# Zero products also into banks that a step will start anew, and another table of due times

## The chip, the cores and the metric

The kernel runs on one core of one Trainium2 chip. The metric is the device time of one execution in microseconds. The kernel before took 186.7 us, the median of three runs (185.85, 186.70 and 187.02).

## The reference

Inputs are `x` (4096 x 64, f32), an adjacency matrix `adj` (4096 x 4096, f32, zeros and ones), a weight (64 x 64) and a bias (64). What is computed:

```python
h = jnp.maximum(_layernorm(x, axis=-1), 0.0)
support = h @ weight
mask = (adj != 0).astype(support.dtype)
rank = jnp.cumsum(mask, axis=1)
deg = rank[:, -1:]
k = jnp.minimum(deg, 100.0)
pos = rank - (deg - k)
w = mask * jnp.where(pos > 0, 0.5 ** (k - pos), 0.0)
return x + (w @ support + bias)
```

So the last neighbour of a row has weight 1, the one ahead of it 1/2, and so on, up to 100 neighbours. `adj` is 64 MiB of the 68.19 MB that the kernel reads, and each element of it has to be turned into a weight before the large product.

## The kernel before

The rows of `adj` are handled in 32 tiles of 128 rows and 4096 columns, 2 MB each. Tiles 0, 1 and 28 to 31 are loaded in two or three pieces (`CUTS`), the others in one. A tile passes through these steps, each a small function:

- `load` (SP's queue) brings it into one of four buffers `a_sb`. It has to wait until the convert of the tile four before has read that buffer.
- `convert` (DVE, L563) makes bytes of the 0/1 numbers, in two halves of 2048 columns; `flip` (DVE, L573) transposes them in blocks of 32.
- `totals` (PE, L581) counts neighbours in blocks, `split` (ACT, L589) copies the counts to `sums`, `suffix` (PE, L602) sums them over all later blocks, `clamp` (DVE, L608) limits the result, `place` (PE, L618 and L622) adds the ranks within a block. `place` fills four banks of PSUM with exponents.
- `weigh` (ACT, L636), four per tile, reads one such bank each and writes the weights `wk` by an exponential. For one quarter of tiles 30 and 31 DVE does this instead (`encode`, L643, and `take`, L647).
- `aggregate` (PE, L656) multiplies the weights of a pair of tiles with `hr`, the support in two parts, in eight steps of four matmuls, adding up in a bank. A bank takes two pairs, that is a group of four tiles (the last group uses two banks).
- `drain` (ACT L671 or DVE L673) takes a finished group out of its bank, `turn_back` (PE, L679) transposes it, `finish` (DVE, L685) adds `x`, `store` writes it out.

Ahead of this, in the first 50 us, a setup computes the layer norm and the support: `turn`, `center`, `spread`, `support` on PE, `turned`, `square`, `relu`, `first` on ACT, `root`, `power`, `scale` (L532), `second` (L542) on DVE.

**The order of the steps.** There is no loop over tiles in the emitted program. `tasks` lists 665 steps with engine, estimated hold and lag, and needs; `plan` puts them in order. At each turn it takes the first open step of every kind, finds when each could start, and among those of the engine with the earliest that can start within `WAIT` (250 ns on PE, 60 on DVE, 150 on ACT, 60 on POOL, 0 on SP) of it, takes the one with the smallest due time from `DUE`. Steps of one kind keep their order. Each engine then runs its steps strictly in the planned order. `plan` also picks the banks: a step that writes a fresh bank gets the one that is free the earliest, and the bank numbers go to it as `homes`.

**Zero products.** `plan` asks for a number of products of zeros ahead of a step on PE, from PE's gap before the step and from the rows it streamed in the last 3.4 us:

```python
idle = max(0, min(int((at - end) * 0.6) // 110, (4200 - recent) // 256))
```

`warm` (L482) issues them: 128 x 256 products of the zero tile `junk` (L484). They need a bank to write. `idle` names it: at first the last bank; after an aggregate the bank and columns of that aggregate, to which zeros are added. A `drain` of the bank that `idle` names empties `idle` (L668), and from then on to the next aggregate `warm` issues nothing.

## Time and profile before

| | |
|---|---|
| median of three runs | 186.7 us |
| the profiled execution, its own time | 187.01 us |
| its span, first to last instruction | 185.0 us |
| busy in the span: PE, DVE, ACT | 165.2, 153.9, 149.5 us |
| DMA, mean over the span | 376 GB/s |
| DMA, 10 to 160 us | some 425 GB/s |
| mean granted TensorE clock | 0.98 |

The span is cut in 40 slices, each a digit of busy tenths for each engine. Groups of instructions carry the line of the kernel, the engine, the output and input tile, the count, the mean time of one, and the idle time just before them with what ended it. A wait written as `[0.33 <-PE bank L581]` means that the engine was idle for 0.33 us and that a PE instruction of line 581 released it.

### The profile page before, as it was taken

The numbers are of one execution on the slowest core, as the hardware profiler recorded it, in microseconds if no ns is written. First come the engines' busy times: TensorE is split into PE (matmuls) and PEld (weight loads), VectorE is DVE, ScalarE is ACT, GpSimd is POOL, SyncE is SP. The second block draws the span as 40 slices with busy tenths as digits, with TensorE's granted clock in tenths as the row PEclk, the third lists the DMA queues.
The fourth block names the chain that finished last, engine by engine and source line by source line (L and its number), as shares of the span: only waits on it lengthen the run. The fifth ranks groups of instructions, "written<-read, shape, count | busy, mean of one in ns | idle before, by whom it ended". The sixth has DMA issues, their size and how long they took to land.

```text
span 185.0 us, 4842 instructions
## 1 busy us (share of the span) xinstructions
PE 165.2 (89%) x2087; PEld 128.4 (69%) x2087; DVE 153.9 (83%) x204; ACT 149.5 (81%) x196; POOL 7.7 (4%) x43
## 2 busy tenths in 40 slices
PE   7999987579799999899999899997499999989992
PEld 5857874267586776687868588776277678777891
DVE  6667299999999999898889698888984989998731
ACT  2476912839699999999999999994896999999931
POOL 7810000000000000000000000000000000000000
PEclk9999999999999999999999999999958999999999
DMA  6999999999999999999999999999999999960020
GB/s 225 420 415 436 429 425 418 441 407 446 414 436 418 427 425 418 436 429 425 425 422 432 418 429 432 418 432 425 429 422 420 413 416 416 414 267 0 4 87 28
DMA packets 6807, 69.55 MB, mean 376 GB/s; under 512 B 898, under 2 KB 1154, under 8 KB 2178
## 3 DMA queue, kind: packets, MB, share of 16 engines
q1 hardware_dynamic: 6786, 69.24, 89.1%
q8 instruction: 16, 0.26, 0.6%
q14 instruction: 5, 0.04, 0.1%
HBM read 68.19 MB, written 1.05 MB: 374 GB/s over the span
## 4 chain that ended last, share of the span: by engine, by line
ACT 29%; PE 26%; DMA 19%; DVE 16%; issue 8%; SPq 0%; ACTq 0%; DVEq 0%
ACT wk L636 23%; DMA a_sb<-in_adj_dram 19%; PE bank L656 15%; DVE m L563 8%; ACT sums L589 4%; PE bank L602 4%; DVE mt L573 3%; PE bank L679 3%; PE bank L622 2%; PE bank L581 2%; PE bank L618 2%; DVE behind L608 1%; DVE wk L532 1%; DVE hr L542 1%; ACT acc_sb L671 1%
## 5 line engine op out<-in xcount | busy, mean ns | idle before, releaser
L636 ACT ACTIVATE wk<-bank 128x1024 fp32r<-128x1024 uint8 (+2 forms) x136 | 122.7, 1067 | 7.9 <-PE bank L622 6.3
L563 DVE TENSOR_SCALAR m<-a_sb 128x2048 uint8<-128x2048 f32 (+1 forms) x66 | 85.7, 1345 | 14.5 <-DMA a_sb<-in_adj_dram 14.3
L656 PE MATMUL bank<-wk,hr 128*128 128x256 f32 x512 | 73.2, 292 | 3.5 <-DVE hr L542 2.5
L656 PEld LDWEIGHTS bank<-wk,hr 128*128 128x128 f32 x512 | 64.4, 192 | 10.3 <-issue 5.0
L573 DVE STREAM_TRANSPOSE mt<-m 128x1024 f32<-128x1024 f32 (+2 forms) x40 | 40.5, 1022 | 0.4
L589 ACT ACTIVATE sums<-bank 128x512 f16<-128x512 uint8 x32 | 21.6, 685 | 7.2 <-PE bank L581 7.2
L608 DVE TENSOR_SCALAR behind<-bank,excess 128x256 f16<-128x256 f32 x32 | 14.8, 466 | 4.4 <-PE bank L602 4.1
L602 PEld LDWEIGHTS <-far 128*128 128x128 f16 x224 | 17.7, 99 | 0.9
L602 PE MATMUL bank<-sums,far 128*128 128x224 f16 (+6 forms) x224 | 18.1, 222 | 0.0
L618 PE MATMUL bank<-behind,where 32*128 32x256 f16 x256 | 14.5, 277 | 3.9 <-DVE behind L608 1.9
L484 PE MATMUL bank<-junk 128*128 128x256 bf16 x93 | 14.7, 299 | 1.2 <-DVE junk L372 1.2
L581 PE MATMUL bank<-mt,band 128*32 128x256 f16 x256 | 13.3, 284 | 2.4 <-DVE mt L573 1.7
L622 PE MATMUL bank<-mt,tri 32*32 32x512 f16 x512 | 14.4, 403 | 0.0
L602 PE MATMUL bank<-sums,near 128*128 128x256 f16 x32 | 9.0, 280 | 4.4 <-ACT sums L589 3.8
L484 PEld LDWEIGHTS <-junk 128*128 128x128 bf16 x93 | 9.0, 106 | 4.8 <-issue 2.0
L618 PEld LDWEIGHTS <-where 32*128 32x128 f16 x256 | 4.7, 92 | 9.8 <-issue 7.4
L581 PEld LDWEIGHTS <-band 128*32 128x32 f16 x256 | 4.5, 95 | 7.9 <-issue 3.8
L622 PEld LDWEIGHTS <-tri 32*32 32x32 f16 x512 | 4.4, 88 | 6.9 <-issue 6.9
L602 PE MATMUL bank<-sums,rest 128*128 128x256 f16 x32 | 8.8, 276 | 0.0
L495 ACT ACTIVATE wk<-bank 64x512 f32<-64x512 f32 x8 | 4.3, 587 | 4.9 <-PE bank L491 4.9
L685 DVE TENSOR_TENSOR xr<-bank,xr 128x256 f32<-128x256 f32 (+1 forms) x9 | 3.5, 389 | 5.6 <-PE bank L679 5.6
L679 PE MATMUL bank<-both,acc_sb 128*128 128x64 f32 x56 | 7.5, 277 | 0.6 <-ACT acc_sb L671 0.6
(95 smaller groups left out, 86.2 us busy)
## 6 DMA issues: line engine op xcount, KB each, us to landing
a_sb<-in_adj_dram SPq DMA_DIRECT2D x26, 2048.0 KB, 16.8
a_sb<-in_adj_dram SPq DMA_DIRECT2D x10, 1024.0 KB, 12.7
a_sb<-in_adj_dram SPq DMA_DIRECT2D x4, 512.0 KB, 14.5
xr<-in_x_dram SPq DMA_DIRECT2D x2, 512.0 KB, 4.8
out_dram<-xr SPq DMA_DIRECT2D x1, 512.0 KB
out_dram<-xr SPq DMA_DIRECT2D x1, 384.0 KB, 2.7
out_dram<-xr SPq DMA_DIRECT2D x2, 64.0 KB, 1.6
w<-in_L_gnn_weight_dram SPq DMA_DIRECT2D x2, 16.0 KB, 9.4
```

The source lines that it names most:

```text
L484: nc.tensor.matmul(idle[0][:, idle[1]:idle[1] + 2 * P], junk[:, :P], junk, start=not accs, stop=not accs, skip_group_check=True)
L563: nc.vector.tensor_scalar(words[n][:, k0 * P:k1 * P, :].rearrange("p (h q) e -> p h e q", q=P), tiles[t][:, (h0 + k0) * W:(h0 + k1) * W].r ...
L573: nc.vector.transpose(to[:, h0:h1], m_v.rearrange("p (h c l) -> p h c l", c=4, l=SUB))
L581: nc.tensor.matmul(tot[SUB * c:SUB * (c + 1), r], band[:, SUB - 12 - 4 * a:2 * SUB - 12 - 4 * a], masks[t][:, c, r, a], start=(a == 0), st ...
L589: nc.scalar.activation(sums8[t][:, :, r], pts.pop((n, "n")).bitcast(U8).rearrange("p (i f) -> p f i", f=4)[:, :2, r], AF.Copy, bias=-136.0)
L602: nc.tensor.matmul(o, l, m, start=(k == 0), stop=(k == len(todo) - 1), skip_group_check=True)
L608: nc.vector.tensor_scalar(behind[n][:, r], pts.pop((n, "s"))[:, r], excess, float(MAX_NEIGH), op0=ALU.subtract, op1=ALU.min)
L618: nc.tensor.matmul(vs[n, j][:, h0:h1, a, :], where[q, a, :], behind[n][q, r], start=(a == 0), stop=False, skip_group_check=True)
L622: nc.tensor.matmul(vs[n, j][SUB * c:SUB * (c + 1), h0:h1], tri[q, q], masks[t][q, c, r, :].rearrange("p (h r) a -> p h a r", r=SUB), start ...
L636: nc.scalar.activation(to[:, :, :, j, :], v[:, :2, x], AF.Exp, scale=-LN2, bias=-38.0 * LN2)
L656: nc.tensor.matmul(accs[g][:, at:at + 2 * P], hr[:, h * 4 + e, :, :].rearrange("p s d -> p (s d)"), wts[u][:, s, 2 * h + a].rearrange("p i ...
L679: nc.tensor.matmul(pts["o", d][:, k, :], sums[d][:, k * P:(k + 1) * P], both, start=True, stop=True)
```

## The change

Two things. First, `warm` no longer stops when `idle` is empty: it then writes its zero products into the first bank of `homes`, the one that the step about to be issued will start anew. To make this possible `homes` is set before `warm` is called. Such products start and stop an accumulation of their own, as those ahead of the first aggregate do. A step without banks of its own still gets none. Second, nearly all due times in `DUE` are others; costs, needs, buffers and the rule of `plan` are as they were. The orders of loads against fetches and of the stores don't change. Of the table only the kinds spoken of below are shown; numbers stand in the order of tiles, for `weigh` four to a tile (more for tile 29, and three per part for tiles 30 and 31).

```diff
@@ DUE @@
...
-    "split": [468, 298, 398, 367, 301, 306, 338, 385, 365, 389, 267, 369, 215, 291, 184, 201, 206, 274, 271, 261, 263,
-    401, 335, 319, 295, 293, 322, 379, 381, 414, 356, 357],
+    "split": [484, 337, 322, 377, 314, 383, 333, 416, 320, 415, 267, 400, 233, 325, 240, 289, 304, 362, 366, 301, 356,
+    381, 251, 262, 264, 252, 265, 293, 360, 358, 359, 363],
-    "totals": [445, 418, 94, 112, 489, 84, 87, 138, 140, 144, 130, 118, 119, 208, 256, 229, 86, 221, 168, 228, 186, 165,
-    145, 164, 197, 179, 49, 45, 63, 71, 73, 479],
+    "totals": [451, 428, 127, 129, 477, 130, 122, 218, 195, 205, 153, 136, 111, 200, 229, 155, 154, 199, 159, 167, 160,
+    117, 175, 80, 62, 61, 75, 59, 68, 46, 112, 49],
-    "suffix": [467, 463, 120, 111, 487, 139, 106, 141, 98, 126, 128, 107, 193, 207, 200, 157, 161, 174, 247, 250, 163,
-    212, 205, 198, 177, 236, 55, 66, 69, 76, 51, 650],
+    "suffix": [464, 458, 219, 173, 491, 208, 152, 183, 124, 179, 158, 143, 228, 238, 214, 191, 184, 215, 168, 178, 115,
+    87, 84, 81, 55, 106, 101, 78, 64, 99, 102, 121],
-    "weigh": [505, 216, 243, 342, 321, 325, 328, 361, 312, 307, 302, 355, 366, 387, 373, 374, 386, 364, 354, 399, 396,
-    394, 362, 345, 392, 340, 384, 280, 390, 391, 284, 276, 242, 189, 265, 289, 375, 219, 241, 257, 292, 204, 255, 187,
-    283, 297, 290, 190, 203, 211, 282, 270, 252, 259, 264, 268, 275, 244, 262, 269, 281, 287, 273, 285, 266, 246, 346,
-    334, 279, 288, 327, 278, 332, 260, 402, 339, 337, 348, 314, 331, 341, 299, 351, 336, 311, 320, 310, 376, 308, 318,
-    323, 315, 294, 316, 329, 317, 304, 248, 305, 330, 382, 417, 286, 296, 370, 406, 383, 388, 371, 393, 377, 416, 359,
-    368, 350, 358, 378, 395, 352, 372, 405, 412, 397, 347, 353, 333, 349, 403, 413, 343, 415, 407, 410, 344, 411, 409],
+    "weigh": [577, 298, 174, 340, 417, 344, 405, 336, 423, 329, 222, 406, 422, 413, 379, 328, 424, 394, 235, 378, 420,
+    425, 371, 312, 427, 334, 242, 271, 419, 414, 278, 309, 389, 280, 206, 319, 426, 286, 316, 305, 421, 318, 225, 310,
+    373, 375, 317, 221, 330, 313, 243, 321, 307, 306, 376, 323, 295, 367, 353, 303, 352, 396, 324, 351, 302, 392, 402,
+    365, 395, 409, 407, 374, 245, 382, 390, 404, 380, 279, 254, 263, 244, 297, 261, 290, 283, 284, 288, 268, 250, 269,
+    259, 277, 258, 253, 270, 266, 247, 273, 274, 294, 276, 272, 296, 275, 339, 255, 327, 368, 361, 364, 372, 369, 335,
+    341, 357, 393, 355, 370, 349, 391, 397, 398, 347, 403, 331, 332, 388, 401, 399, 346, 350, 385, 345, 342, 387, 348],
...
@@ -480,8 +480,11 @@
     idle = [banks[BANKS - 1], 2 * P]
 
     def warm(n):
-        for i in range(n if idle else 0):
-            nc.tensor.matmul(idle[0][:, idle[1]:idle[1] + 2 * P], junk[:, :P], junk, start=not accs, stop=not accs, skip_group_check=True)
+
+        to = idle or [banks[i] for i in homes[:1]] + [0]
+        for i in range(n if len(to) > 1 else 0):
+            keep = bool(idle and accs)
+            nc.tensor.matmul(to[0][:, to[1]:to[1] + 2 * P], junk[:, :P], junk, start=not keep, stop=not keep, skip_group_check=True)
 
     pxs, ns = {}, {}
 
@@ -693,8 +696,8 @@
         support, scale, first, second, convert, flip, totals, split, suffix, clamp, place, weigh, encode, take, aggregate,
         drain, turn_back, finish, store)}
     for at, spare, f, args, given in plan():
+        homes[:] = given
         warm(spare)
-        homes[:] = given
         does[f](*args)
 
     last = {}
```

Of the other kinds, `power` goes from 495 to 507, `scale` from 500, 454, 449, 507 to 504, 476, 472, 509.

## Prediction

> **What bounds the kernel now.** I read the slices of the page first, for the engine that is full in each stage and for the clock.

> ```profile
> PE   7999987579799999899999899997499999989992
> ...
> ACT  2476912839699999999999999994896999999931
> ...
> PEclk9999999999999999999999999999958999999999
> DMA  6999999999999999999999999999999999960020
> ```

> One digit is 4.6 us. Loads fill the DMA engines up to slice 35 and end in the 36th. ACT is full from about 50 us on, but for slices 28 to 31. PE has a dip in slices 28 and 29 (124.9 to 134.1 us), and right after it the only dip of its clock. So I cut that stretch into steps of 3.4 us; columns are length, then busy time (count) of PE, weight loads, DVE, ACT and POOL, then clock, DMA share and GB/s.

> ```profile
> 124.90:128.30 3.40, 3.40 (x41) 2.96 (x41) 2.48 (x3) 2.01 (x4) 0.00 (x0) 1.00 1.01 424
> 128.30:131.70 3.40, 1.85 (x56) 0.75 (x57) 3.40 (x6) 1.43 (x2) 0.00 (x0) 1.00 1.01 429
> 131.70:135.10 3.40, 1.49 (x14) 1.33 (x11) 3.37 (x3) 3.40 (x5) 0.00 (x0) 0.74 1.00 424
> 135.10:138.50 3.40, 3.40 (x20) 2.56 (x20) 2.86 (x4) 3.07 (x5) 0.00 (x0) 0.50 1.00 424
> 138.50:141.90 3.40, 3.40 (x45) 2.47 (x45) 0.81 (x3) 2.72 (x4) 0.00 (x0) 0.75 1.00 424
> ```

> PE is half idle from 128.3 to 133.7; then it is fully busy at half clock until about 140. Finer steps put the half clock from 133.7 to 140.1, 6.4 us, so 3.2 us of PE's work are lost. In it ACT and DVE starve. From the timeline of ACT, three waits on PE, and of DVE one:

> ```profile
> 136.70 0.60 ACT L589 ACTIVATE sums<-bank 128x512 f16<-128x512 uint8 x1 [0.33 <-PE bank L581]
> 139.81 2.86 ACT L636 ACTIVATE wk<-bank 128x1024 fp32r<-128x1024 uint8 x3 [0.68 <-PE bank L622]
> 143.68 0.60 ACT L589 ACTIVATE sums<-bank 128x512 f16<-128x512 uint8 x1 [1.01 <-PE bank L581]
> ...
> 141.36 0.48 DVE L608 TENSOR_SCALAR behind<-bank,excess 128x256 f16<-128x256 f32 x1 [2.59 <-PE bank L602]
> ```

> ACT loses 0.33 + 0.68 + 1.01 = 2.02 us. After 144.3 it has no hole above 0.2 us until its last weigh ends at 177.58, though the last load lands at about 166.4 (the DMA share falls to zero there). So ACT, with PE some microseconds behind it, sets the end, not the loads; 2 us lost at 140 are 2 us at 185.

> Ahead of the dip ACT has a larger hole of another origin:

> ```profile
> 130.27 2.85 ACT L636 ACTIVATE wk<-bank 128x1024 fp32r<-128x1024 uint8 x3 [3.36 <-PE bank L622]
> ```

> split(21) stands on ACT behind all four weighs of tile 20. Only then can suffix, clamp and place of tile 21 run, one after another on PE, DVE and PE, before ACT has a weigh again. PE idles in the same hole, and that costs the clock.

> **Why PE had no filler there.** The planner's rule, followed through for the kernel before, asks for 108 zero products; the page has 93:

> ```profile
> L484 PE MATMUL bank<-junk 128*128 128x256 bf16 x93 | 14.7, 299 | 1.2 <-DVE junk L372 1.2
> ```

> The missing 15 are 2 ahead of place(21), 3 ahead of totals(23) and 10 ahead of suffix(23). drain(4), at 125.74 on ACT, clears `idle`, and it stays empty until aggregate(10, 0), at 134.84 in the trace. They fall just into the stretch that loses its clock.

> [...] here the starts of `near` and `rest` (256 columns) at 127.53 and 127.64 are 110 ns apart. [...]

> **The change, part by part.**

> Filler allowed after a drain: were the order as before, 15 products more. At 110 ns they are 1.65 us of PE. Ten lie ahead of suffix(23), 1.1 us, inside PE's wait of 1.91 us for `sums`; the others lie in PE's waits of 1.11 and 0.44 us. Cost: nothing while those waits and a free bank cover it; if the bank is read late, up to 1.1 us for the ten. They raise PE's work in 131.7 to 135.1 from 1.49 to about 2.6 us, and some earlier. That it suffices is my choice: from 30 to 40 us PE is busy 6.67 of 10 us, 2.3 in 3.4, at clock 1.00. Gain: the 2.02 us of ACT, bounded by 0 (it doesn't suffice) and by PE's 3.2 us. The 3.36 us hole stays: the new table still gives split(21) 381 against 244 to 297 for the weighs of tile 20.

> What is late next: the landing. The last convert (0.73 us) could start at 166.4 instead of 167.81, so flips end 1.4 us sooner than 169.2, at 167.8. clamp(30), behind them, takes 0.48, place(30) 0.7, then ACT needs 3 x 1.03 us for weigh(30) before tile 31: 167.8 + 0.5 + 0.7 + 3.1 + 0.2 of gaps is 172.3, against 174.34 now. So the tail can follow by 2.0 us and hardly more, which is also what ACT gives.

> Order: the diff changes nearly every due time, no duration, and the fetches, loads and stores keep their order on SP. A due time decides only between steps that can start within 250, 60, 150 or 60 ns (PE, DVE, ACT, POOL) of the earliest, so most of the order follows the data. Counting from the tables where split(n) is due after every weigh of tile n-1: tiles 2, 3, 9, 11, 13, 21, 29, 31 before; 9 and 21 after. That is fewer chances for a hole. In the tail totals(31) goes from due 479 to 49 and suffix(31) from 650 to 121, ahead of most aggregates; in the trace they stood 1.1 us (168.99 to 170.11, eight matmuls of L656) and 0.5 us behind such. Together 1.6 us at most, but weigh(30) on ACT covers it except for the gaps of 0.16 and 0.17 us before the last split and weigh. I count 0.2 us. A loss is open too: the trace of before can't bound how the new order fills 20 to 50 us, where ACT is busy only 16.55 of 30 us. I bound it by one tile of ACT work either way: 4 x 1.067 + 0.685 = 4.95 us.

> Sum: 2.0 + 0.2 = 2.2 us off a span of 185.0, so 182.8. Around the span lie 2.0 us (187.0 - 185.0). That execution is 0.3 us above the median of the three, so against 186.7 the forecast is 184.5 us.

> **The rivals.**

> One: the clock is repaired and the tail closes up (45%): 184.5, its own range 183.6 to 185.6; 185.6 is half the gain.

> Two, slower: a later ramp of ACT (27%). Place: 20 to 50 us, where DVE is full (27.68 of 30 us) and ACT waits for DVE's scale (3.58 and 2.64 us) and for hr (1.39 us). If setup steps there are ordered so that one tile's ACT work slips past 50 us, 4.95 us come on top of a stage in which ACT is full; 186.7 - 2.2 + 4.95 = 189.5. It decides against the change as soon as ACT's busy time in 20 to 50 falls by more than 2.2 us. For it: DVE is saturated there, and new due times for every tile's convert against scale and second. Against: these steps keep similar ranks (power 495 to 507, scale 449-507 to 472-509).

> Three: no effect (16%): the half clock comes all the same, in this hole or another, with the waits unchanged: 186.7, give or take 1. [...]

> Four: the order also closes the 3.36 us hole, and clamp(30) gets ahead of the last flips (12%). Then place(31) limits: flips at 167.8 plus totals 0.4, split 0.6, suffix 0.75, clamp 0.5, place 0.75 and 0.5 of gaps is 171.3, instead of 174.25: 3.0 off, 183.7; if ACT also ramps earlier no more, as the landing holds. Order of DVE in the last 5 us could give another 0.7: 183.

> **How the numbers follow.** 1% is 1.9 us, about what a measurement of this kernel can tell from no change: faster is below 184.8, slower above 188.6. Case one puts 60% below 184.8 (27) and the rest within (18); case four is all faster (12); case two is 24 slower and 3 within; case three is 14 within and 1 each side. Faster 40%, same 35%, slower 25%. The range from 183.2 to 189.5 leaves out the upper half of case two and a little of case four.

> **What would show it.** Right: PEclk without a dip; L484 above 93, some of them writing banks between a drain and the next aggregate; ACT's waits on PE in 130 to 145 gone; the last weigh ends near 175.5. Wrong: ACT's busy time in 20 to 50 below 14.4 us; a dip in another slice; zero products directly ahead of a step with a wait on a bank's reader; L563 waiting for a buffer rather than for DMA, or a DMA slice below 400 GB/s before 160 us, which would mean that loads waited for DVE.

## The result and the profile after

The changed kernel takes 184.76 us (median of four runs, 184.69 to 184.88) against 186.86 us for the kernel before (185.85 to 187.05); the ratio is 0.990, 95% interval 0.986 to 0.994. The span of the profiled execution is 182.8 us, 2.2 less than before. The kernel before spreads more than the changed one: in the later rounds below its median lay between 185.94 and 186.49 us, so 1.5 us is as fair a size of the gain as 2.1.

The slices of the page of the changed kernel, 4.57 us each:

```profile
PE   7999999598899899989999898997999989999992
...
ACT  2576801928999999999999999649999999999931
PEclk9999699969999999999999999999999999999999
DMA  6999999999999999999999999999999999992020
```

The dip of the clock behind 130 us is gone. There is one in slice 5 and another in slice 9, in the setup, where the kernel before had none in its profiled execution. ACT still has a hole, now in slices 26 and 27, some 9 us earlier than before.

The same steps of 3.4 us as in the prediction, for the changed kernel, with the same columns:

```profile
124.90:128.30 3.40, 2.83 (x47) 1.97 (x46) 2.66 (x3) 3.40 (x5) 0.00 (x0) 1.00 0.98 414
128.30:131.70 3.40, 3.40 (x50) 3.02 (x37) 2.79 (x4) 3.40 (x5) 0.00 (x0) 1.00 1.03 439
131.70:135.10 3.40, 3.15 (x47) 2.41 (x47) 3.40 (x4) 3.40 (x5) 0.00 (x0) 1.00 0.98 414
135.10:138.50 3.40, 3.38 (x51) 2.40 (x49) 2.99 (x4) 3.40 (x5) 0.00 (x0) 1.00 1.03 434
138.50:141.90 3.40, 3.40 (x55) 2.60 (x54) 2.79 (x4) 3.40 (x6) 0.00 (x0) 1.00 0.96 410
```

The clock is at 1.00 and ACT is full in all five (3.40 of 3.40). What became of the hole is seen in the timeline of PE of the changed kernel (lines are 3 higher than before: L487 is a zero product, L584 `totals`, L605 `suffix`, L659 `aggregate`; a cut is marked by dots):

```profile
112.28 4.03 PE L659 MATMUL bank<-wk,hr 128*128 128x256 f32 x32
...
118.36 0.55 PE L605 MATMUL bank<-sums,far 128*128 128x224 f16 x7
118.77 1.91 PE L487 MATMUL bank<-junk 128*128 128x256 bf16 x16
120.65 0.41 PE L584 MATMUL bank<-mt,band 128*32 128x256 f16 x8
```

and in ACT's timeline, at the same place:

```profile
121.17 0.60 ACT L592 ACTIVATE sums<-bank 128x512 f16<-128x512 uint8 x1 [3.72 <-PE bank L584]
```

ACT waits 3.72 us, and during that wait 16 zero products keep PE busy. They don't need the changed rule: at this place `idle` names the bank of an aggregate, since the drain just past (drain(3)) was of an older group. Of the 116 zero products of the changed kernel only 3 fall where `idle` is empty (2 ahead of aggregate(4, 0), 1 ahead of aggregate(12, 0)). So the diff's two parts had to be told apart.

### The profile page after: what moved, and what is told of

Same layout as the page of the kernel before. It is cut to its first block, busy times and chain, and to the rows that moved or that the text cites. A ratio compares the mean times of both kernels' runs of the same rounds, so it can differ in the third digit from the quotient of the medians.

```text
span 182.8 us, 4886 instructions
## 1 busy us (share of the span) xinstructions
PE 167.9 (92%) x2110; PEld 130.4 (71%) x2110; DVE 154.2 (84%) x204; ACT 149.1 (82%) x196; POOL 7.8 (4%) x43
## 4 chain that ended last, share of the span: by engine, by line
DMA 51%; DVE 23%; PE 20%; issue 3%; ACT 1%; SPq 0%; POOL 0%; DVEq 0%; POOLq 0%; ACTq 0%
DMA a_sb<-in_adj_dram 51%; DVE m L566 13%; PE bank L659 8%; DVE mt L576 5%; PE bank L532 3%; PE bank L605 2%; PE bank L682 2%; DVE behind L611 1%; DVE wk L535 1%; PE bank L625 1%; PE bank L584 1%; PE bank L621 1%; PE bank L514 1%; DVE hr L545 1%; DVE xr L688 1%
## 5 line engine op out<-in xcount | busy, mean ns | idle before, releaser
L659 PE MATMUL bank<-wk,hr 128*128 128x256 f32 x512 | 74.3, 290 | 2.5 <-ACT wk L639 1.5
L659 PEld LDWEIGHTS bank<-wk,hr 128*128 128x128 f32 x512 | 64.1, 189 | 10.4 <-issue 5.7
L592 ACT ACTIVATE sums<-bank 128x512 f16<-128x512 uint8 x32 | 20.6, 650 | 8.9 <-PE bank L584 8.8
L487 PE MATMUL bank<-junk 128*128 128x256 bf16 x116 | 18.0, 297 | 1.2 <-DVE junk L372 1.2
L621 PE MATMUL bank<-behind,where 32*128 32x256 f16 x256 | 14.4, 272 | 4.5 <-ACT wk L639 2.3
L605 PEld LDWEIGHTS <-far 128*128 128x128 f16 x224 | 17.7, 99 | 0.9
L605 PE MATMUL bank<-sums,far 128*128 128x224 f16 (+6 forms) x224 | 18.1, 222 | 0.0
L584 PE MATMUL bank<-mt,band 128*32 128x256 f16 x256 | 13.3, 284 | 2.8 <-DVE mt L576 2.5
L611 DVE TENSOR_SCALAR behind<-bank,excess 128x256 f16<-128x256 f32 x32 | 14.8, 468 | 0.0
L487 PEld LDWEIGHTS <-junk 128*128 128x128 bf16 x116 | 11.1, 105 | 5.2 <-issue 2.2
L584 PEld LDWEIGHTS <-band 128*32 128x32 f16 x256 | 4.6, 94 | 8.4 <-issue 4.6
L605 PE MATMUL bank<-sums,near 128*128 128x256 f16 x32 | 9.1, 284 | 0.1
L605 PE MATMUL bank<-sums,rest 128*128 128x256 f16 x32 | 8.9, 277 | 0.0
L542 ACT ACTIVATE hr<-wk 128x512 fp32r<-128x512 f32 x4 | 2.3, 623 | 7.1 <-DVE wk L535 7.1
## 6 DMA issues: line engine op xcount, KB each, us to landing
a_sb<-in_adj_dram SPq DMA_DIRECT2D x10, 1024.0 KB, 14.5
```

Of the source, the lines that this page charges most:

```text
L487: nc.tensor.matmul(to[0][:, to[1]:to[1] + 2 * P], junk[:, :P], junk, start=not keep, stop=not keep, skip_group_check=True)
L584: nc.tensor.matmul(tot[SUB * c:SUB * (c + 1), r], band[:, SUB - 12 - 4 * a:2 * SUB - 12 - 4 * a], masks[t][:, c, r, a], start=(a == 0), st ...
L592: nc.scalar.activation(sums8[t][:, :, r], pts.pop((n, "n")).bitcast(U8).rearrange("p (i f) -> p f i", f=4)[:, :2, r], AF.Copy, bias=-136.0)
L605: nc.tensor.matmul(o, l, m, start=(k == 0), stop=(k == len(todo) - 1), skip_group_check=True)
L611: nc.vector.tensor_scalar(behind[n][:, r], pts.pop((n, "s"))[:, r], excess, float(MAX_NEIGH), op0=ALU.subtract, op1=ALU.min)
L621: nc.tensor.matmul(vs[n, j][:, h0:h1, a, :], where[q, a, :], behind[n][q, r], start=(a == 0), stop=False, skip_group_check=True)
```

## The experiments

**Which part of the change does it.** Theory A says that the gain is the clock, whoever keeps it; theory B that it is the order. The edit of the first is the code of the diff without its table, that of the second the table without the code.

```diff
 e1: DUE as before
+        to = idle or [banks[i] for i in homes[:1]] + [0]
...
 e2: DUE as after
-        to = idle or [banks[i] for i in homes[:1]] + [0]
...
```

> The due times of before, with the changed rule for zero products alone: 108 of them instead of 93. Theory A (the gain is the clock): no dip of the clock near 133 to 140 us, ACT's three waits of 2.02 us on PE gone, about 184.7 us, ratio 0.989. Theory B (the gain is the new order, the zero products do nothing that matters): 186.7 us, ratio 1.00.

> The due times of after, with the rule of before: 113 zero products instead of 116, since only 3 of those that the new order asks for fall where the old rule issues none (2 ahead of aggregate(4, 0), 1 ahead of aggregate(12, 0)). Theories A and B both: 184.8 us, no dip after 100 us. Theory C (the new rule is needed in the new order too): a dip near 150 us and 185.5 us or more.

The old table with the new rule: 184.87 us (184.63 to 188.49, six runs, one of them above 185), ratio 0.992 (0.989 to 0.995) to the kernel before, which had 186.30 in that round. The new table with the old rule: 184.76 us (184.67 to 184.94), ratio 0.992 (0.989 to 0.995). Each part gives the whole gain alone, and together they give no more: 184.76. In the first, the 15 missing products are there (108), and they do what was forecast; its windows are

```profile
128.30:131.70 3.40, 2.17 (x56) 0.94 (x53) 3.38 (x6) 1.43 (x2) 0.00 (x0) 1.00 1.04 443
131.70:135.10 3.40, 3.01 (x33) 2.34 (x31) 3.37 (x3) 3.40 (x5) 0.00 (x0) 1.00 0.96 405
135.10:138.50 3.40, 3.40 (x52) 2.39 (x52) 2.82 (x4) 3.40 (x6) 0.00 (x0) 1.00 1.04 439
```

with PE at 3.01 us instead of 1.49 in the second line and the clock at 1.00 throughout. ACT's three waits of 2.02 us are gone, and its hole of 3.36 us is still there, 3.27 us long. So theory B falls as stated; but A alone doesn't say why the new order needs no new rule. The reading is that it moved the idle stretch to a place where the old rule fills it; the next run asks for that.

**Is it the filling?** Here the 25 zero products that the new order has in its idle stretch are left out.

```diff
-        warm(spare)
+        warm(spare if not 118000 < at < 130000 else 0)
```

> After, without the 25 zero products that its order has at 118 to 126 us (16 ahead of totals(21), 6 ahead of place(20), 3 ahead of totals(22)). Theory A: PE falls idle there, the clock drops to half for 3 to 7 us after 120, and the time is 186 to 187 us. Theory B: no more than 0.2 us from 184.8.

Median 185.00 us, ratio 0.994 (0.992 to 0.996); but 22 runs spread from 184.26 to 187.30, 8 of them above 186. With the products the same order gave 184.69 to 184.88. The windows of this kernel:

```profile
118.40:121.80 3.40, 1.41 (x24) 0.72 (x22) 3.40 (x6) 0.23 (x1) 0.00 (x0) 0.85 1.06 453
121.80:125.20 3.40, 2.94 (x53) 1.55 (x49) 3.40 (x4) 2.89 (x4) 0.00 (x0) 0.64 0.96 410
125.20:128.60 3.40, 2.72 (x60) 1.94 (x44) 2.65 (x3) 3.40 (x6) 0.00 (x0) 1.00 1.04 434
```

PE idles, and the half clock comes, from 120.81 to 124.22 us in this execution, which cost 0.3 us of span (183.1). The expectation of 186 to 187 us held for a third of the runs only. The mean granted clock of each run sorts them without an overlap: the eleven at 0.972 and below took 185.07 to 187.30 us, the eleven at 0.976 and above 184.26 to 184.94. Only one of the runs has a trace; read by the mean clock, the same kernel loses the clock without the products in half of its executions (11 of 22), and those are the slow ones: the products are an insurance in this order, while in the old one their lack cost even the fastest of 33 runs (185.69) about a microsecond.

**How many are needed?** The old table with the new rule, half of the 15.

```diff
-        warm(spare)
+        warm(spare // 2 if 128000 < at < 134000 else spare)
```

> The due times of before with the changed rule, but 7 zero products (1, 1 and 5) in place of 15 (2, 3 and 10) ahead of place(21), totals(23) and suffix(23). If about 2.3 us of PE work in 3.4 us keep the clock, as the stretch from 30 to 40 us suggested, 7 are too few in most executions (1.49 + 0.7 to 0.8 us): the half clock comes back in part of the runs, and they spread from 184.7 to 187. If fewer do: 184.8, no spread.

185.04 us (184.61 to 185.12, six runs), ratio 0.991 (0.989 to 0.993): no spread, and the clock is at 1.00 from 124.9 to 142.2 us of the profiled execution. Seven are enough. Their work had been counted as 0.11 us each; in the windows of this kernel PE is busy

```profile
128.30:131.70 3.40, 2.61 (x66) 1.22 (x64) 3.39 (x6) 1.62 (x2) 0.00 (x0) 1.00 1.01 429
131.70:135.10 3.40, 2.24 (x26) 1.78 (x26) 3.37 (x4) 3.40 (x6) 0.00 (x0) 1.00 0.99 414
```

so the 2.24 us that the expectation feared to be too few were enough. They can't be set against 1.85 and 1.49 us in the kernel before: 1.43 of the 1.49 us came after its clock had dropped. The last section cuts the time where the clock changes.

**What caps the gain?** ACT's hole was the largest loss left. In the old order, with the changed rule, four steps were moved ahead by hand so that tile 21 gets through to its weighs in time (banks and zero products follow from the planner's rule).

```diff
+MOVES = [
+    (('split', 21), ('weigh', 20, 0, 0)),
+    (('suffix', 21), ('aggregate', 9, 3)),
+    (('clamp', 21), ('flip', 24)),
+    (('place', 21), ('totals', 22)),
+]
```

> The due times of before with the changed rule, and four steps of tile 21 moved ahead by hand: split(21) ahead of weigh(20, 0), suffix(21) ahead of aggregate(9, 3), clamp(21) ahead of flip(24), place(21) ahead of totals(22). ACT's hole of 3.36 us near 127 to 130 us should close and the clock hold. If ACT's lost time counts in full: 186.7 - 2.0 - 3.4 = 181.3 us. Theory A with its cap (the tail follows by 2.0 to 2.3 us, since the last load lands at 166.4): 184.5, and ACT then waits for PE or DVE elsewhere, for 3 us in all.

184.85 us (184.38 to 186.40, 12 runs), ratio 0.993 (0.990 to 0.995). The hole is closed (the longest wait of ACT there is 0.69 us), and nothing comes of it. Two of the 12 runs lie above 186 us, at a mean clock of 0.970 and 0.972, so this order may lose the clock at times; no trace of such a run was kept. ACT's lost time doesn't count in full: the 5.4 us of hole and slow clock are worth no more than the 2 us of the slow clock alone. Next, single engines and the landing were relieved in the last 35 us of the changed kernel, by leaving out a piece of work and with it a part of the result.

```diff
 e5, in weigh
+        if (n, j) in ((27, 0), (28, 0)):
+            return nc.gpsimd.memset(to[:, :, :, j, :].bitcast(F32), 0.0)
 e6, in load and convert
+        if n not in (38, 39):
             nc.sync.dma_start(...)
+        src = 0 if n in (38, 39) else h0
 e9, in aggregate
+        if u == 13 and h in (2, 3, 4, 5):
+            return
 e10, in convert
+        if n in (34, 36):
+            return nc.gpsimd.memset(words[n][:, k0 * P:k1 * P, :], 64)
```

> After, but weigh(27, 0) and weigh(28, 0) are left out of ACT: GpSimd, idle there, writes zeros into their part of the weights, so the output lacks these neighbours. ACT has 2 x 1.03 = 2.06 us less to do between 150 and 165 us. Theory L (the tail is held by the landing of the last load and the chain behind it): no more than 0.4 us off 184.8, and ACT waits for PE near 168. Theory R (the tail is held by ACT's backlog): 2 us off, 182.7.

> After, without the last two loads of tile 31 (512 KB each, 2.5 us at 425 GB/s); their converts read the first columns of that tile instead, so DVE, PE and ACT do the same work on other data. Theory L: the flips can end earlier, by 0.3 us (DVE's only wait for DMA after 160 us in after) up to 2.5 us, and the end follows, 182.5 to 184.5. Theory R: nothing, 184.8.

> Both of the two edits before in one kernel. If the landing and ACT's backlog hold the tail together, each alone gives little and both together 1 to 2 us: 183 to 184. Theory L alone: as without the last loads. Theory R alone: as with ACT relieved. If neither is it (DVE or PE full in the last 20 us): 184.6 or more in all three.

> After, without aggregate(13, 2) to (13, 5), so that tiles 26 and 27 lack the products of half their columns: 16 matmuls of L659, about 2.1 us of PE between 160 and 168 us. In the three runs before this PE had no gap from 159 to 178 us, whatever was relieved. Theory P (the tail is PE's own remaining work): 1.5 to 2.1 us off 184.8, about 183.0. Theory D (the tail is DVE's work on the last tiles and the chain behind their flips): 0.5 us or less, and PE shows gaps before the last totals, suffix and place instead.

> After, with two of three converts of tile 30 left out of DVE (GpSimd writes the bytes for no neighbours, so tile 30 is mostly empty): 2.0 us less on DVE between 159 and 163 us. Theory P: nothing, 184.6 to 184.9, the flips end at most 0.3 us earlier since the last convert waits for its load. Theory D: up to 2 us off.

> Both edits. If PE and DVE hold the tail together, each alone gives less than half of 2 us and both give 1 to 2. Theory P: as with PE relieved alone. Theory D: as with DVE relieved alone.

Medians: ACT relieved 184.40, last loads left out 184.64, both 184.85; PE relieved 184.69, DVE relieved 185.05, PE and DVE 185.10. None of the theories named there holds: 2 us less of any of them, or of two, is worth 0.4 us at best. Even the 0.4 us of ACT isn't shown to be the edit's: at 141 us, ahead of all these edits, the same split starts at 141.01 to 141.78 us in these kernels. And DVE was relieved by less than 2 us: with GpSimd writing the bytes, the two converts at 155.1 us took 3.48 us in the kernel with PE and DVE relieved, against 2.69 in the changed kernel. What all have in common is seen when two moments are read from their timelines: the start of the convert of tile 31's first piece (piece 37), and of totals(31).

| kernel | convert of piece 37 | totals(31) | span | span less totals(31) |
|---|---|---|---|---|
| before | 165.29 | 170.11 | 185.0 | 14.9 |
| after | 163.86 | 167.88 | 182.8 | 14.9 |
| old table, new rule | 163.43 | 167.76 | 182.6 | 14.8 |
| hole closed | 163.43 | 167.65 | 182.5 | 14.9 |
| ACT relieved | 163.41 | 167.50 | 182.4 | 14.9 |
| last loads left out | 163.74 | 167.76 | 182.7 | 14.9 |
| PE relieved | 163.73 | 167.88 | 182.8 | 14.9 |
| PE and DVE relieved | 163.85 | 168.49 | 183.4 | 14.9 |

The time after totals(31) is the same in all: 14.9 us, also in the traces not listed here. Before it three paths meet. DVE, in the timeline of the changed kernel:

```profile
163.86 2.06 DVE L566 TENSOR_SCALAR m<-a_sb 128x2048 uint8<-128x2048 f32 x2 [0.29 <-DMA a_sb<-in_adj_dram]
165.82 0.68 DVE L576 STREAM_TRANSPOSE mt<-m 128x512 f32<-128x512 f32 x1
166.44 0.72 DVE L566 TENSOR_SCALAR m<-a_sb 128x1024 uint8<-128x1024 f32 x1
167.05 0.75 DVE L576 STREAM_TRANSPOSE mt<-m 128x256 f32<-128x256 f32 x2
```

The convert waits for the load of piece 37; then tile 31 is 3.9 us of DVE work without a gap, to 167.8. The loads left out were the two behind it, whose landing that work hides. PE comes to totals(31) after eight matmuls of aggregate(14, 0) and (14, 1), without a gap, at 167.88. With PE relieved these matmuls wait for ACT instead, and totals(31) starts at the same 167.88:

```profile
166.73 1.21 PE L661 MATMUL bank<-wk,hr 128*128 128x256 f32 x8 [0.70 <-ACT wk L639]
167.88 0.41 PE L584 MATMUL bank<-mt,band 128*32 128x256 f16 x8
```

So the load with DVE's 3.9 us behind it, PE's queue, and ACT's weights of tile 29 all reach totals(31) within half a microsecond of each other. With the cover of one gone, the next holds. No convert of piece 37 started before 163.34 us in any trace. The change could not move the loads: from 10 to 160 us the DMA engines are full and move 425 GB/s in both kernels, before and after (the last three numbers are clock, DMA share and GB/s).

```profile
10.00:160.00 150.00, 135.53 (x1773) 103.63 (x1770) 131.56 (x148) 127.56 (x161) 0.00 (x0) 0.98 1.01 425
10.00:160.00 150.00, 139.85 (x1826) 106.77 (x1823) 133.50 (x150) 128.83 (x162) 0.00 (x0) 0.98 1.01 425
```

What it did is to let the engines follow closer behind them: the convert of piece 37 came at 165.29 us before and comes at 163.86. A run in which that load comes earlier, with all three engines relieved, wasn't made; that it is the last pin is read from the waits, not shown by an edit.

**A step of the fixed chain taken out.** In the chain of waits of the changed kernel the end reads

```profile
174.00 4.29 PE bank L659 x36
178.29 0.41 PE bank L682 x4
178.70 0.02 issue
178.72 0.48 ACT acc_part L674
179.20 0.04 issue
179.25 0.67 PE bank L682 x4
```

Here drain(8) on ACT comes only after turn_back(7), which reads the tile `acc_part` that drain(8) is to write: two drains share one buffer.

```diff
-        ... else opool.tile([P, V], F32, name="acc_part")
+        ... else opool.tile([P, V], F32, name=f"acc_part{i0}")
```

> After, with a tile of its own for each of the last two drains, so that drain(8) on ACT need not wait until turn_back(7) has read the one tile acc_part. Theory E (the end is the start of totals(31) plus a fixed chain of 14.9 us, as in the 13 traces so far): drain(8) starts 0.41 us earlier, beside turn_back(7), turn_back(8) follows it at once, the chain becomes 14.5 us; about 184.35 us. Rival: another step of that chain, such as a store, takes up the 0.41 us: 184.76.

184.37 us (184.00 to 184.47, six runs), ratio 0.991 (0.988 to 0.994) to the kernel before, which had 185.94 in that round. In its timelines turn_back(8) follows turn_back(7) at 0.72 us instead of 1.12:

```profile
177.75 0.55 PE L682 MATMUL bank<-both,acc_part 128*128 128x64 f32 x4
178.47 0.66 PE L682 MATMUL bank<-both,acc_part 128*128 128x64 f32 x4 [0.17 <-ACT acc_part L674]
```

totals(31) started at 167.50 and the span is 182.0: the chain is 14.5 us, as theory E said. The other 0.4 us of span, an earlier totals(31), isn't the edit's. That this version is faster than the changed kernel (184.69 to 184.88) is likely but not shown side by side, since the two ran in different rounds.

## Why the prediction was right, and where its steps were not

The size was right: 184.5 forecast, 184.76 measured, span 182.8 forecast and measured. That the clock is what the change repairs was right too. That the sum came out so well is in part luck: two of its supports, that ACT sets the end and that the last load caps the gain, didn't hold. Point by point:

- **The clock.** That the half clock came from 15 products that `warm` dropped is shown by the old table with the new rule: 15 products more, the clock at 1.00 from 115 to 145.6 us, 184.87 us against 186.30 in its round. That they would cost nothing where they were put holds too: ACT's weigh behind the hole starts at 130.27 us with and without them. Two readings were off. The half clock began at 133.37 and ended at 140.19 us, so it lasted 6.8 us, not 6.4. And of the 1.49 us of work from 131.7 to 135.1 us, which the 15 products were to raise to 2.6, 1.43 came after it had begun.
- **Which part brings it.** The sum gave 2.0 us to the rule and 0.2 to the order. In fact either alone gives all. The changed rule is nearly idle in the new order (3 of 116 products), and the order brings the gain by putting the idle stretch where the old rule works. The sum came out because both repair the same loss.
- **The order's 0.2 us in the tail** failed. totals(31) with its due time of 49 stands behind the same eight matmuls as with 479 (166.76 to 167.88 in after). A due time decides only among steps ready together, and the planner's estimates had them not ready.
- **The hole that stays** stayed in size, 3.72 us, but 9 us earlier and by another chain: suffix(19) behind 32 matmuls of aggregate, and its clamp behind a convert, which had waited 0.91 us for its load, and a flip on DVE. The reading from split(21) against the weighs of tile 20 named the wrong place.
- **"2 us lost at 140 are 2 us at 185"** was right in effect, not in its reason. ACT doesn't set the end alone: 2.06 us less for it to do gave at most 0.4 us, its closed hole nothing.
- **The cap by the landing** held in its number only: the last convert was forecast to start at 166.4 and started at 166.44. But with the last two loads left out it still started at 166.30. What pins it is the first load of tile 31 with DVE's work behind it, not the last, and PE and ACT arrive at the same moment.
- **No dip of the clock** was wrong: the changed kernel has two in the setup, at 0.50 from 19.08 to 22.50 and from 36.15 to 39.56 us, where the kernel before has none. A mean clock as low as its 0.981 need not show in the time: with the old table and the new rule five runs at 0.981 to 1.000 took 184.63 to 184.92 us, the one at 1.000 took 184.86. From 66 to 117 us DVE waits for its loads nine times in the changed kernel, 5.6 us in all; that would cover what the setup loses, but no experiment shows it.
- **Later ramp of ACT, the slower rival**: ACT is busy 16.96 us in 20 to 50 us, 0.41 more than before, so it didn't happen. No effect, the third case, didn't happen either.

## What to carry to other kernels

When the clock drops behind an idle stretch, ask first why the filler wasn't there; a handful of products can be enough (seven here), and moving the stretch to where filler works does as well (184.76 us, against 184.87 with the filler put in). Before adding up what several engines lost, look for the step where their paths meet: measure from there to the end in several variants, and if that time is constant (14.9 us here), what comes ahead counts only up to the next path. Then shorten the constant part: a second buffer for the last two drains took 0.4 us off it. And read a small difference between two kernels beside the spread of the kernel that both are compared with, and from the same round.

## What the runs showed of the hardware

```profile
129.95:133.37 3.42, 1.36 (x48) 0.56 (x33) 3.42 (x4) 3.10 (x4) 0.00 (x0) 1.00 1.02 436
133.37:136.78 3.41, 3.11 (x22) 2.30 (x22) 2.84 (x4) 3.08 (x5) 0.00 (x0) 0.50 0.99 413
136.78:140.19 3.41, 3.41 (x34) 2.34 (x35) 1.99 (x2) 2.73 (x4) 0.00 (x0) 0.50 1.03 437
...
117.40:120.81 3.41, 1.46 (x21) 1.40 (x20) 3.41 (x5) 0.00 (x0) 0.00 (x0) 1.00 1.02 432
120.81:124.22 3.41, 3.36 (x44) 1.58 (x44) 3.41 (x5) 2.13 (x3) 0.00 (x0) 0.50 1.05 447
...
130.89:134.30 3.41, 2.08 (x23) 1.33 (x22) 3.37 (x4) 3.41 (x6) 0.00 (x0) 1.00 1.00 423
```

- **Losing the clock.** Of all such steps at full clock between 45 and 175 us in the traces before and after, the one with the least PE work, 1.36 us, was followed by the half clock, and no other, from 2.31 us up. Without the zeros it followed a step of 1.46 us; with half of them the stretch of 2.08 us kept the clock. After 175 us, where PE runs out of work, it followed a step of 0.66 us in the kernel before. Busy time isn't the whole measure: in the setup of the changed kernel the half clock followed a step of 1.64 us, from 32.73 us on, but also one of 3.11 us, from 15.67 us on, in which 16 matmuls of 2 columns take 1.93 us.
- **Getting it back.** The half clock lasted two steps in the kernel before (6.8 us) and one without the zeros (3.4 us). Before, a step at half clock with 3.11 us of PE work was followed by another, and one with 3.41 us by the full clock; so were those of 3.41 and 3.31 us in the setup after, and the one of 3.36 us without the zeros.
- **Chance.** An idle stretch of the same program isn't equally costly in each execution: 184.26 to 187.30 us in 22 runs without filler, 184.69 to 184.88 in four with it. Counted back in such steps, the first begins at 0.25 us in the trace before and at 2.02 us in the one after, so the same stretch could fall into one step or be shared by two; that this is the reason was not shown, since only one of the 22 runs has a trace.
